# Layer 1's linear attention: q formed transposed and squared at eviction, its norm applied at the output rows, x (Wv W_out) in one product with k

## The chip, the cores and the metric

The kernel runs on one core of one Trainium2 chip. The metric is the device time of one execution in microseconds. The median of three timed runs of the kernel before is 815.91 us (812.31 to 816.70). Engines are named as in the profile: PE is TensorE (PEld its weight loads), DVE is VectorE, ACT is ScalarE, POOL is GpSimd, SP is the queue from which most DMAs are issued.

## The reference

The program is a small vision tower: a tokenizer, then layer 0 (attention and a mixture of six experts), then layer 1 (linear attention and a gated mixture with a shared MLP). The change is in the linear attention of layer 1:

```python
def _L1_attn_ref(x, W_qkv, b_qkv, W_out, b_out):
    b, N, C = x.shape
    qkv = x @ W_qkv + b_qkv
    q, k, v = jnp.split(qkv, 3, axis=2)
    q = q - jnp.mean(q, axis=2, keepdims=True)
    k = k - jnp.mean(k, axis=2, keepdims=True)
    q2 = q * q
    k2 = k * k
    q2s = jnp.sum(q2, axis=2, keepdims=True)
    k2s = jnp.sum(k2, axis=2, keepdims=True)
    k2 = _l2_normalize(k2 / (k2s + EPS_DIV), axis=-2)
    q2 = _l2_normalize(q2 / (q2s + EPS_DIV), axis=-1)
    kv = jnp.einsum('bnc,bnd->bcd', k2, v)
    t2 = jnp.einsum('bnc,bcd->bnd', q2, kv) / math.sqrt(N)
    attn = v + t2
    return attn @ W_out + b_out
```

Here x is the layer norm of h, and the result is added to h. There are 4 images; each has 2352 tokens that are three equal copies of 784, so the kernel computes 784 rows per image and writes each three times. C is 256. Everything is float32; a product of the code appears as two matmuls in the trace.

Two facts are used. Since q2 is normalised along its own row, dividing it by its sum first changes almost nothing, and its norm is one number per token. And (v + t2) W_out is x (Wv W_out) plus q2 (kv W_out) plus constants, so v itself need not be formed.

## The kernel before

The 28 tiles of 112 tokens (TT) are cut into eight units, for each image one of four tiles and one of three (`units`); the odd units have three. The names below stand with their lines in the kernel before.

- `fetch(u)` (L1360) gathers the experts' rows of unit u from DRAM, one indirect DMA of GpSimd per tile and choice; `stats_one` and `normalise` (L1383 to L1406) add them to h, take the statistics and write the normalised rows `xa`; `residual` (L1413) adds the constant row `bres` to h. `ys`, the gathered rows, has three buffers.
- `x_t(u)` transposes `xa` on TensorE (`pt`, L297) and copies the result to `lxT` (half on ScalarE, L81, half on VectorE, L83).
- `q_k(u, j0, j1)` multiplies each tile by the centred 512 columns of q and k (`pqk`, L1574). VectorE adds the bias (L1578); ScalarE squares both halves with a row sum (L1582) and squares q's half once more into `junk` for the sum of fourth powers (L1583).
- `scales(u)` takes the root of that sum (L1598) and the reciprocals (L1602), multiplies k's half on ScalarE into `uk` (L1606) and q's half on VectorE in place (L1607), and squares `uk` into `sq` (L1611). `fold(u)` adds `sq` up (L1618 to L1623).
- `q_t(u)` transposes q (`pt<-ident,qk`, L297) and copies it to `lqT`.
- `k_x(b)`, once an image: the column norms `pn`, `kn` (L1635 to L1642), the product `pukx` of uk with the rows xa (L1648) and its scaled copy `g` (L1652). `g_t(b)` turns g (`pgT`, L1662, copied at L1665); `kv_out(b)` multiplies it by Wvo (`pkvo`, L1674) and writes `kvo` on VectorE (L1678).
- `rows_out(u)`: for two tiles at a time one PSUM tile `pout` takes lxT times Wvo (L1689) and, on top, lqT times kvo (L1694); VectorE adds it to h (L1700).
- `layer1_weights()` makes Wvo = Wv W_out and the constant row: transposes `pwv` (L598), a copy `WvT` on VectorE (L602), products `pwvo` (L607), copies `Wvo` on ScalarE (L611), and the bias part `pbvo` (L618 to L621). It is called in step u = 1, after that unit's q and k.

A loop over u = 0 to 9 strings these together; a unit's rows go out two steps after its q and k were made. In this stage the order of the instructions on each engine is made by a scheduler, from the program's order and its own estimate of when operands are ready; it is fixed when the kernel is built. The expert blocks just before (`hidden`, `rows_back`, L1165 to L1199) have the order of VectorE and of the SP queue written out by hand; `centred_weights()` is called in them. PSUM has a pool of seven banks (`ps_tile`) and one further bank (`psum_s`, one buffer) for `pn` and the small gate products.

Of the kernel before, what the change touches and what calls it, by code (L numbers as in the profile page):

```python
# [60 lines left out]
def tile_vit_tower(ctx: ExitStack, tc: tile.TileContext, a: dict, out: bass.AP):  # L61
# [515 lines left out]
    def centred_weights():  # L577
        qkw = Wqkv[:, :, : 2 * D].rearrange("p c (i d) -> p c i d", i=2)
        mean = w1p.tile([P, 2, 2], F32, tag="mean", name="mean")
        nc.vector.tensor_reduce(mean, qkw, AX.X, ALU.add)  # L580
        nc.vector.tensor_scalar(mean, mean, 1.0 / D, None, ALU.mult)
        nc.vector.tensor_tensor(
            qkw, qkw, mean.unsqueeze(3).to_broadcast([P, 2, 2, D]), ALU.subtract
        )
        qkb = bqkv[:, : 2 * D].rearrange("p (i d) -> p i d", i=2)
        meanb = w1p.tile([TT, 2], F32, tag="meanb", name="meanb")
        nc.vector.tensor_reduce(meanb, qkb, AX.X, ALU.add)
        nc.vector.tensor_scalar(meanb, meanb, 1.0 / D, None, ALU.mult)
# [749 lines left out]
    bout = spread(w1p, "bout", a["L1_attn_b_out"], nc.sync)  # L1338

# [94 lines left out]
    with tc.manual_schedule(engines={mybir.EngineType.DVE, mybir.EngineType.SP}):  # L1434
        own_weights(NEARLY)
        turned(NEARLY)
        for i in range(NEARLY, NBLK + 1):
# [117 lines left out]
    lin = linear.enter_context(tc.tile_pool(name="lin", bufs=2, reuse_waits="tile"))  # L1555
    sumsof = {}

    def q_k(u, j0, j1):

        n = units[u][2]  # L1560
        xT = xTs[u]
        if j0 == 0:
            qks[u] = lin.tile([TT, GT, 2 * D], F32, tag="qk", name="qk")
            sumsof[u] = (
                small.tile([TT, GT, 2], F32, tag="ss", name="ss"),
                small.tile([TT, GT], F32, tag="s4", name="s4"),
            )
        qk = qks[u]
        ss, s4 = sumsof[u]
        junk = lin.tile([TT, D], F32, tag="junk", name="junk", bufs=1)  # L1570
        for j in range(j0, min(j1, n)):
            pqk = ps_tile("pqk")[:TT]
            for c in range(2):
                nc.tensor.matmul(  # L1574
                    pqk, xT[:, c, cut(j, 1)], Wqkv[:, c, : 2 * D],
                    start=(c == 0), stop=(c == 1),
                )
            nc.vector.tensor_tensor(qk[:, j, :], pqk, bqkv[:, : 2 * D], ALU.add)  # L1578

            for i in range(2):  # L1580
                half = qk[:, j, i * D : (i + 1) * D]
                nc.scalar.activation(half, half, AF.Square, accum_out=ss[:, j, i : i + 1])  # L1582
            nc.scalar.activation(junk, qk[:, j, :D], AF.Square, accum_out=s4[:, j : j + 1])  # L1583
            if u:
                stats_one(u + 1, j)
        if j1 >= n and u:
            if u + 1 < len(units) and units[u + 1][2] > n:
                stats_one(u + 1, n)
            normalise(u + 1)

    def scales(u):

        b, j0, n = units[u]
        qk = qks[u]
        ss, s4 = sumsof.pop(u)

        nc.vector.tensor_scalar(ss[:, :n], ss[:, :n], 1e-7, None, ALU.add)
        nc.scalar.activation(s4[:, :n], s4[:, :n], AF.Sqrt, bias=zero[:TT])  # L1598
        nc.vector.scalar_tensor_tensor(
            ss[:, :n, 0], ss[:, :n, 0], 1e-12, s4[:, :n], ALU.mult, ALU.max  # L1600
        )
        nc.vector.reciprocal(ss[:, :n], ss[:, :n])  # L1602
        uk = uks[u] = lin.tile([TT, GT, D], F32, tag="uk", name="uk", bufs=3)
        sq = lin.tile([TT, GT, D], F32, tag="sq", name="sq", bufs=1)
        for j in range(n):
            nc.scalar.activation(uk[:, j, :], qk[:, j, D:], AF.Copy, scale=ss[:, j, 1:2])  # L1606
            nc.vector.tensor_scalar(  # L1607
                qk[:, j, :D], qk[:, j, :D], ss[:, j, 0:1], None, ALU.mult
            )
        for j in range(n):  # L1610
# [3 lines left out]
    def fold(u, sq):  # L1614
# [4 lines left out]
        else:  # L1619
# [62 lines left out]
    def rows_out(u):  # L1682
        b, j0, n = units[u]
        xT, qT, kvo = xTs.pop(u), qTs.pop(u), kvos[b]
        for two in halves(range(n)):
            pm = ps_tile("pout")[:TT].rearrange("p (t d) -> p t d", t=2)
            for i, j in enumerate(two):
                for c in range(2):
                    nc.tensor.matmul(  # L1689
                        pm[:, i, :], xT[:, c, cut(j, 1)], Wvo[:, c, :],  # L1690
                        start=(c == 0), stop=False,
                    )
                for c in range(2):
                    nc.tensor.matmul(  # L1694
                        pm[:, i, :], qT[:, c, cut(j, 1)], kvo[:, c, :],
                        start=False, stop=(c == 1),
                    )
# [7 lines left out]
    for u in range(len(units) + 2):  # L1705
        b, odd = divmod(u - 2, 2)
        one_image = u >= 2 and not odd
        if u == 0:
            fetch(3)
            x_t(1)  # L1710
            q_k(0, 0, GT)
            squares[0] = scales(0)
            fold(0, squares.pop(0))
            continue
        if u < len(units):
# [3 lines left out]
        if one_image:  # L1719
            k_x(b)  # L1720
            q_t(u - 1)
        if u == 2:
# [129 lines left out]
```

## Time and profile before

| | us |
|---|---|
| timed runs, median of 3 (lowest, highest) | 815.91 (812.31, 816.70) |
| the profiled execution's own time | 849.85 |
| its span, first to last instruction | 848.1 |

The profiled execution's mean granted TensorE clock is 0.954 of full speed. By stretches of the trace, TensorE is busy for 335 of the first 400 us, 108 of the 110 between 400 and 510, and 137 of the last 144 (the gated mixture). The linear attention of layer 1 lies between about 518 and 704 us.

Some groups of that stage (busy us in all, mean ns of one):

| line | engine | what | count | busy us | mean ns |
|---|---|---|---|---|---|
| L1574 | PE | pqk, 512 columns | 112 | 50.0 | 595 |
| L1689 | PE | pout from Wvo, 256 columns | 107 | 27.8 | 380 |
| L1694 | PE | pout from kvo, 256 columns | 104 | 27.1 | 382 |
| L1648 | PE | pukx, 258 columns | 112 | 29.0 | 415 |
| L1582 | ACT | Square of q and of k with row sum | 56 | 22.8 | 407 |
| L1583 | ACT | Square for the fourth powers | 28 | 11.3 | 402 |
| L1578 | DVE | bias added to q and k, 512 columns | 28 | 19.2 | 688 |
| L1607 | DVE | q scaled, 256 columns | 28 | 8.2 | 353 |

Busy times on one engine overlap: matmuls are pipelined, and an instruction's end reaches into the next one's start. The distance from start to start is what a long row of them costs. A few matmul records are missing from the trace (112 would be expected for both rows of pout).

### The profile page before, as it was taken

The page shows a single profiled execution, that of the slowest core. Times are in us where ns is not written, and L with a number is a line of the kernel's source. Part 1 is how long each engine was busy: PE and PEld are TensorE (multiplying, and loading weights), DVE is VectorE, ACT ScalarE, POOL GpSimd, SP SyncE. Part 2 cuts the span into 40 slices and gives each one's busy share as a digit, 9 for nine tenths or more (in the row PEclk, how much of TensorE's full clock was granted, in tenths as well). Part 3 has the DMA queues.
Part 4 walks back from the last instruction along what each step waited for, and adds up shares of the span by engine and source line. Part 5 has one row for each costly group of instructions (what it writes and reads, how often), then busy time and mean ns, then how long its engine had stood idle before and what let it go on. Part 6 is the DMA issues. An engine that isn't in the chain of part 4 may idle for free. (4 is left out here: it accounts for less than half of the span.)

```text
span 848.1 us, 11129 instructions
## 1 busy us (share of the span) xinstructions
PE 746.0 (88%) x3669; PEld 525.4 (62%) x3669; DVE 515.1 (61%) x1619; ACT 318.2 (38%) x758; POOL 129.3 (15%) x151
## 2 busy tenths in 40 slices
PE   2879988999788788799999999348999999999996
PEld 2758765555465466678878885335767675555553
DVE  4369886585787874346445655358995745544441
ACT  1333535455547573242222323323564612222221
POOL 5100000000024605430030022744000000000000
PEclk9999999999999988799999999759999999999999
DMA  8999990000001293332342224311000001333333
GB/s 197 360 421 419 419 384 0 1 0 1 1 22 55 82 367 95 103 127 75 100 131 88 94 88 137 93 52 55 1 2 0 1 3 27 100 101 101 99 100 100
DMA packets 58286, 97.52 MB, mean 115 GB/s; under 512 B 14590, under 2 KB 48564, under 8 KB 53364
## 3 DMA queue, kind: packets, MB, share of 16 engines
q1 hardware_dynamic: 51100, 80.78, 27.7%
q0 software_dynamic: 6224, 14.13, 5.8%
q10 hardware_dynamic: 904, 1.89, 0.9%
q8 instruction: 29, 0.48, 0.2%
q14 instruction: 29, 0.24, 0.1%
HBM read 31.04 MB, written 65.74 MB: 114 GB/s over the span
## 5 line engine op out<-in xcount | busy, mean ns | idle before, releaser
L901 POOL DMA_INDIRECT xrows<-xn,pos x56 | 59.9, 1070 | 282.4 <-ACT kq L665 233.2
L1369 POOL DMA_INDIRECT ys<-yrows,pos x56 | 54.3, 969 | 163.5 <-DMA yrows<-yb 134.0
L1173 PE MATMUL pb<-xTb,own 128*128 128x256 f32 x240 | 60.3, 396 | 7.0 <-DVE hb L1181 2.1
L1190 PE MATMUL pyb<-own,hb 128*128 128x256 f32 x240 | 59.4, 392 | 4.4 <-ACT hb L1179 4.4
L1173 PE MATMUL pb<-hb,own 128*128 128x256 f32 x240 | 58.8, 388 | 0.3 <-DVE hb L1181 0.3
L1179 ACT ACTIVATE hb<-pb,own 128x256 f32<-128x256 f32 x74 | 34.7, 473 | 61.7 <-PE pb L1173 42.1
L1173 PEld LDWEIGHTS pb<-xTb,own 128*128 128x128 f32 x240 | 45.5, 198 | 16.7 <-ACT xTb L1163 3.8
L1190 PEld LDWEIGHTS pyb<-own,hb 128*128 128x128 f32 x240 | 46.9, 197 | 12.0 <-ACT hb L1179 5.2
L297 PE MATMUL pt<-ident,xn 112*128 112x112 f32 x280 | 42.2, 281 | 12.4 <-DVE xn L482 6.9
L1574 PE MATMUL pqk<-Wqkv,lxT 128*112 128x512 f32 x112 | 50.0, 595 | 0.5 <-ACT lxT L81 0.5
L297 PEld LDWEIGHTS pt<-ident,xn 112*128 112x128 f32 x280 | 32.4, 148 | 26.4 <-issue 9.1
L1173 PEld LDWEIGHTS pb<-hb,own 128*128 128x128 f32 x240 | 44.5, 195 | 6.2 <-DVE hb L1181 0.7
L1196 DVE TENSOR_TENSOR yb<-pyb,eb 128x512 f32<-128x512 f32 x30 | 20.7, 691 | 45.5 <-PE pyb L1190 35.3
L306 PE MATMUL pe<-xT,eW 128*128 128x448 f32 x112 | 45.2, 546 | 0.0
L1648 PE MATMUL pukx<-xa,uk 112*128 112x258 f32 x112 | 29.0, 415 | 18.5 <-ACT uk L1606 18.5
L1163 ACT COPY xTb<-ptb 128x512 f32<-128x512 f32 x30 | 17.5, 583 | 73.8 <-PE ptb L1159 65.2
L1181 DVE TENSOR_SCALAR hb<-pb,own 128x256 f32<-128x256 f32 x46 | 22.2, 482 | 30.9 <-PE pb L1173 29.6
L1648 PEld LDWEIGHTS pukx<-xa,uk 112*128 112x128 f32 x112 | 22.7, 208 | 22.3 <-issue 18.8
L317 PE MATMUL pwo<-Wo,oT 128*112 128x256 f32 x112 | 29.0, 413 | 7.6 <-DVE oT L730 6.7
L1574 PEld LDWEIGHTS pqk<-Wqkv,lxT 128*112 128x112 f32 x112 | 19.2, 177 | 25.2 <-issue 22.7
L690 DVE SCALAR_TENSOR_TENSOR prod<-kq 128x784 f32<-128x784 f32 x32 | 30.4, 971 | 7.2 <-ACT kq L665 5.0
L1582 ACT ACTIVATE qk<-qk 112x256 f32<-112x256 f32 x56 | 22.8, 407 | 28.1 <-DVE qk L1578 23.8
(339 smaller groups left out, 1525.4 us busy)
## 6 DMA issues: line engine op xcount, KB each, us to landing
xrows<-nothing SPq DMA_DIRECT2D x19, 1024.0 KB
yrows<-nothing SPq DMA_DIRECT2D x19, 1024.0 KB
out_dram<-h SPq DMA_DIRECT2D x26, 336.0 KB
xb<-xrows SPq DMA_DIRECT2D x30, 256.0 KB
yrows<-yb SPq DMA_DIRECT2D x30, 256.0 KB
ew<-in_L_ffn_expert_w_dram SPq DMA_DIRECT2D x6, 768.0 KB
wb<-wd SPq DMA_DIRECT2D x28, 112.0 KB
img<-in_x_dram ACTq DMA_DIRECT2D x2, 588.0 KB
```

The lines of the kernel that those rows point to most:

```text
L297: nc.tensor.transpose(pt[:, j * TT : (j + 1) * TT], xn[:, j, c * P : (c + 1) * P], ident[:TT, :TT])
L306: nc.tensor.matmul(pm[: wcols.stop - wcols.start, :n], w[:, c, wcols], xT(c), start=(c == 0), stop=(c == chunks - 1),)
L317: nc.tensor.matmul(pm[:, i, :], xT(c, t), w[:, c, :], start=(c == 0), stop=(c == chunks - 1))
L690: nc.vector.scalar_tensor_tensor(prod, qTs[s][:, o, :], 1.0, kT[:, o, t * SEQ : (t + 1) * SEQ], ALU.mult, ALU.mult, accum_out=atts[s][:, o ...
L901: put = nc.gpsimd.indirect_dma_start(out=xrows[:, :], out_offset=bass.IndirectOffsetOnAxis(ap=pos[:, k, t0 + j : t0 + j + 1], axis=0), in_ ...
L1173: nc.tensor.matmul(pm, wm[:, c, o * P : (o + 1) * P], src[:, c, :], start=(c == 0), stop=(c == 1),)
L1179: nc.scalar.activation(dst[:, o, :], pm, AF.Relu, bias=b)
L1190: nc.tensor.matmul(pm[:, t, :], src[:, c, t * P : (t + 1) * P], wm[:, c, :], start=(c == 0), stop=(c == 1),)
L1369: got = nc.gpsimd.indirect_dma_start(out=y[:, j, k, :], out_offset=None, in_=yrows[:, :], in_offset=bass.IndirectOffsetOnAxis(ap=pos[:, k, ...
L1574: nc.tensor.matmul(pqk, xT[:, c, cut(j, 1)], Wqkv[:, c, : 2 * D], start=(c == 0), stop=(c == 1),)
L1582: nc.scalar.activation(half, half, AF.Square, accum_out=ss[:, j, i : i + 1])
L1648: nc.tensor.matmul(pg, uks[u][:, k, c * P : (c + 1) * P], xas[u % 4][:, k, : D + 2], start=(j == 0), stop=(j == TPI - 1),)
```

## The change

q and k are no longer one product.

- `k_of(u)` makes k alone. In unit 0, where Wvo doesn't exist yet, it is a product of 256 columns for two tiles at a time; in all later units one of 512 columns, 256 of k and 256 of x Wvo. For this Wvo is kept in the place of Wv in `Wqkv`. VectorE adds k's bias and, in a second instruction, adds the x Wvo half straight to h. Of the Squares with row sum one is left per tile (k's).
- `q_of(u)` makes q transposed (the weights' columns are stationary, lxT moves): two halves of 128 rows by up to 448 tokens. ScalarE evicts each with a Square and a bias column `bq` into `lqT`; one more Square makes `q4`. The transposes of q, their copies and q's scaling on VectorE are gone.
- `norms(u)` sums q4 over the 256 channels with a matrix of ones, four tiles in the four quarters of one PSUM tile, copies it out on ScalarE, turns it with a small matmul, and takes root, maximum and reciprocal into `rq`, one number per token. It is called one step later.
- `rows_out(u)` keeps only the product of lqT with kvo; VectorE multiplies it by rq and adds it to h, tile by tile. Unit 0 alone still does its x Wvo product there.
- `layer1_weights` is called in step 0 instead of step 1, its copy `WvT` moves from VectorE to ScalarE, and its bias columns `bvs` are made earlier (`bias_columns`, in the expert blocks, where `centred_weights` now also makes `bq`).

```diff
--- before.py
+++ after.py
@@ -589,8 +589,21 @@
         nc.vector.tensor_tensor(
             qkb, qkb, meanb.unsqueeze(2).to_broadcast([TT, 2, D]), ALU.subtract
         )
-    def layer1_weights():
+        pb = ps_tile("pbq")
+        for c in range(2):
+            nc.tensor.matmul(
+                pb[:, c : c + 1], bqkv[:1, c * P : (c + 1) * P], ones[:1], start=True, stop=True
+            )
+        nc.vector.tensor_copy(bq, pb[:, :2])
+    def bias_columns():
+        bvs = w1p.tile([P, 2, P], F32, tag="bvs", name="bvs")
+        for k in range(2):
+            nc.vector.tensor_copy(bvs[:, k, :], col("bv", k).to_broadcast([P, P]))
+        return bvs
+    def layer1_weights(bvs):
         WvT = w1p.tile([P, 2, D], F32, tag="WvT", name="WvT")
         pt = ps_tile("pwv").rearrange("p (k i) -> p k i", k=2)
         for k in range(2):
@@ -599,8 +612,8 @@
                     pt[:, k, c * P : (c + 1) * P],
                     Wqkv[:, c, 2 * D + k * P : 2 * D + (k + 1) * P], ident,
                 )
-        nc.vector.tensor_copy(WvT, pt)
-        Wvo = w1p.tile([P, 2, D], F32, tag="Wvo", name="Wvo")
+        nc.scalar.copy(WvT, pt)
+        Wvo = Wqkv[:, :, 2 * D :]
         for c in range(2):
             pw = ps_tile("pwvo")[:, :D]
             for k in range(2):
@@ -609,9 +622,6 @@
                     start=(k == 0), stop=(k == 1),
                 )
             nc.scalar.copy(Wvo[:, c, :], pw)
-        bvs = w1p.tile([P, 2, P], F32, tag="bvs", name="bvs")
-        for k in range(2):
-            nc.vector.tensor_copy(bvs[:, k, :], col("bv", k).to_broadcast([P, P]))
         bvo = w1p.tile([P, D], F32, tag="bvo", name="bvo")
         pw = ps_tile("pbvo")[:, :D]
         for k in range(2):
...
+    bq = w1p.tile([P, 2], F32, tag="bq", name="bq")
...
@@ -1445,6 +1460,7 @@
                 hidden(i, 1)
             if i == NEARLY + 1:
                 centred_weights()
+                bvs = bias_columns()
             for u in range(3):
                 if i - 1 == after[u]:
                     fetch(u)
@@ -1553,60 +1569,92 @@
     late = [early]
 
     lin = linear.enter_context(tc.tile_pool(name="lin", bufs=2, reuse_waits="tile"))
-    sumsof = {}
-    def q_k(u, j0, j1):
-        n = units[u][2]
+    sumsof, q4s, rqs, with_v = {}, {}, {}, set()
+    ones32 = lin.tile([P, 32], F32, tag="ones32", name="ones32", bufs=1)
+    nc.vector.memset(ones32, 1.0)
+    def k_of(u):
+        b, j0, n = units[u]
+        if lw:
+            with_v.add(u)
         xT = xTs[u]
...
+        kr = qks[u] = lin.tile([TT, GT, D], F32, tag="kr", name="kr")
+        ss = sumsof[u] = small.tile([TT, GT], F32, tag="ss", name="ss")
+        for two in halves(range(n)):
+            if not lw:
+                pk = mm_rows(two, lambda c, j: xT[:, c, cut(j, 1)], Wqkv[:, :, D : 2 * D], "pk")
+                nc.vector.tensor_tensor(
+                    kr[:, two[0] : two[-1] + 1, :], pk, over(bqkv[:, D : 2 * D], len(two)),
+                    ALU.add,
+                )
+            for j in two:
+                if lw:
+                    pk = ps_tile("pk")[:TT]
+                    for c in range(2):
+                        nc.tensor.matmul(
+                            pk, xT[:, c, cut(j, 1)], Wqkv[:, c, D:], start=(c == 0), stop=(c == 1)
+                        )
+                    nc.vector.tensor_tensor(kr[:, j, :], pk[:, :D], bqkv[:, D : 2 * D], ALU.add)
+                    ht = h[:, b * TPI + j0 + j, :]
+                    nc.vector.tensor_tensor(ht, pk[:, D:], ht, ALU.add)
+                nc.scalar.activation(
+                    kr[:, j, :], kr[:, j, :], AF.Square, accum_out=ss[:, j : j + 1]
+                )
+                if u:
+                    stats_one(u + 1, j)
+        if u:
             if u + 1 < len(units) and units[u + 1][2] > n:
                 stats_one(u + 1, n)
             normalise(u + 1)
 
+    def q_of(u):
+        n = units[u][2]
+        qT = qTs[u] = lin.tile([P, 2, GN], F32, tag="lqT", name="lqT", bufs=4)
+        q4 = q4s[u] = lin.tile([P, 2, GN], F32, tag="q4", name="q4", bufs=1)
+        for o in range(2):
+            pq = mm_t(
+                n * TT, Wqkv, slice(o * P, (o + 1) * P), lambda c: xTs[u][:, c, : n * TT], "pq1"
+            )
+            nc.scalar.activation(qT[:, o, : n * TT], pq, AF.Square, bias=bq[:, o : o + 1])
+        nc.scalar.activation(q4[:, :, : n * TT], qT[:, :, : n * TT], AF.Square)
+    def norms(u):
+        n = units[u][2]
+        q4 = q4s.pop(u)
+        pg = psum_s.tile([P, 512], F32, tag="pss", name="pq4")[: 32 * n, :TT]
+        for c in range(2):
+            for j in range(n):
+                nc.tensor.matmul(
+                    pg[32 * j : 32 * (j + 1), :], ones32, q4[:, c, cut(j, 1)],
+                    start=(c == 0), stop=(c == 1),
+                )
+        qn = small.tile([P, TT], F32, tag="qn", name="qn", bufs=2)[: 32 * n]
+        nc.scalar.copy(qn, pg)
+        pr = psum_s.tile([P, 512], F32, tag="pss", name="pqn")[:TT, :n]
+        nc.tensor.matmul(
+            pr, qn, ident.rearrange("p (j e) -> p j e", e=32)[: 32 * n, :n, 0],
+            start=True, stop=True,
+        )
+        r = rqs[u] = small.tile([TT, GT], F32, tag="rq", name="rq", bufs=4)
+        nc.scalar.activation(r[:, :n], pr, AF.Sqrt, bias=zero[:TT])
+        nc.vector.tensor_scalar(r[:, :n], r[:, :n], 1e-19, None, ALU.max)
+        nc.vector.reciprocal(r[:, :n], r[:, :n])
     def scales(u):
 
         b, j0, n = units[u]
-        qk = qks[u]
-        ss, s4 = sumsof.pop(u)
+        kr = qks.pop(u)
+        ss = sumsof.pop(u)
         nc.vector.tensor_scalar(ss[:, :n], ss[:, :n], 1e-7, None, ALU.add)
-        nc.scalar.activation(s4[:, :n], s4[:, :n], AF.Sqrt, bias=zero[:TT])
-        nc.vector.scalar_tensor_tensor(
-            ss[:, :n, 0], ss[:, :n, 0], 1e-12, s4[:, :n], ALU.mult, ALU.max
-        )
         nc.vector.reciprocal(ss[:, :n], ss[:, :n])
         uk = uks[u] = lin.tile([TT, GT, D], F32, tag="uk", name="uk", bufs=3)
         sq = lin.tile([TT, GT, D], F32, tag="sq", name="sq", bufs=1)
         for j in range(n):
-            nc.scalar.activation(uk[:, j, :], qk[:, j, D:], AF.Copy, scale=ss[:, j, 1:2])
-            nc.vector.tensor_scalar(
-                qk[:, j, :D], qk[:, j, :D], ss[:, j, 0:1], None, ALU.mult
-            )
+            nc.scalar.activation(uk[:, j, :], kr[:, j, :], AF.Copy, scale=ss[:, j : j + 1])
         for j in range(n):
             nc.scalar.activation(sq[:, j, :], uk[:, j, :], AF.Square)
         return sq
@@ -1621,11 +1669,6 @@
             nc.vector.tensor_tensor(acc, acc, sq[:, 0:2, :], ALU.add)
             nc.vector.tensor_tensor(acc[:, 0, :], acc[:, 0, :], sq[:, 2, :], ALU.add)
             nc.vector.tensor_tensor(acc[:, 0, :], acc[:, 0, :], acc[:, 1, :], ALU.add)
-    def q_t(u):
-        n = units[u][2]
-        qT = qTs[u] = lin.tile([P, 2, GN], F32, tag="lqT", name="lqT", bufs=3)
-        transposed(qks.pop(u), n, lambda c, pt: copy_out(qT[:, c, : n * TT], pt))
 
     def k_x(b):
 
@@ -1681,23 +1724,18 @@
 
     def rows_out(u):
         b, j0, n = units[u]
-        xT, qT, kvo = xTs.pop(u), qTs.pop(u), kvos[b]
+        xT, qT, kvo, r = xTs.pop(u), qTs.pop(u), kvos[b], rqs.pop(u)
         for two in halves(range(n)):
...
             t = b * TPI + j0 + two[0]
             ht = h[:, t : t + len(two), :]
-            nc.vector.tensor_tensor(ht, pm[:, : len(two), :], ht, ALU.add)
+            if u not in with_v:
+                pm = mm_rows(two, lambda c, j: xT[:, c, cut(j, 1)], Wvo, "pxo")
+                nc.vector.tensor_tensor(ht, pm, ht, ALU.add)
+            pq = mm_rows(two, lambda c, j: qT[:, c, cut(j, 1)], kvo, "pqo")
+            for i, j in enumerate(two):
+                nc.vector.scalar_tensor_tensor(
+                    ht[:, i, :], pq[:, i, :], r[:, j : j + 1], ht[:, i, :], ALU.mult, ALU.add
+                )
@@ -1708,9 +1746,12 @@
         if u == 0:
             fetch(3)
             x_t(1)
-            q_k(0, 0, GT)
+            k_of(0)
+            q_of(0)
             squares[0] = scales(0)
             fold(0, squares.pop(0))
+            lw.extend(layer1_weights(bvs))
+            Wvo, bvo = lw[:2]
             continue
         if u < len(units):
             fetch(u + 3)
@@ -1718,21 +1759,20 @@
             shared = shared1(0)
         if one_image:
             k_x(b)
-            q_t(u - 1)
+        if u == len(units):
+            norms(u - 1)
         if u == 2:
             gT = g_t(0)
             kv_out(0, gT)
             rows_out(0)
             x_t(2)
         if u < len(units):
-            q_k(u, 0, 2)
+            k_of(u)
+            norms(u - 1)
         if one_image and b:
             gT = g_t(b)
         if u < len(units):
-            q_k(u, 2, GT)
-            if u == 1:
-                lw.extend(layer1_weights())
-                Wvo, bvo = lw[:2]
+            q_of(u)
             squares[u] = scales(u)
         if one_image and b:
             kv_out(b, gT)
@@ -1743,14 +1783,12 @@
         if 2 <= u < len(units) - 1:
             x_t(u + 1)
         if u == 3:
-            for k in range(3):
+            for k in range(2):
                 residual(k)
         if u >= 2 and (b or odd):
             rows_out(u - 2)
         if u < len(units):
             fold(u, squares.pop(u))
-            if u % 2:
-                q_t(u - 1)
     linear.close()
 
     with tc.tile_pool(name="ffn1", bufs=2) as work:
```

More of the change, by code (lines that the diff above doesn't have):

```diff
@@ L1555, in tile_vit_tower @@
     lin = linear.enter_context(tc.tile_pool(name="lin", bufs=2, reuse_waits="tile"))
-    sumsof = {}
-    def q_k(u, j0, j1):
-        n = units[u][2]
-        xT = xTs[u]
[L1562 to L1566, printed above, removed]
-            )
-        qk = qks[u]
[L1569 to L1576, printed above, removed]
-                )
[L1578 to L1586, printed above, removed]
@@ L1589, in q_k @@
             normalise(u + 1)
+    def q_of(u):
[29 more added lines that the diff above has]
+        nc.vector.reciprocal(r[:, :n], r[:, :n])
     def scales(u):
         b, j0, n = units[u]
-        qk = qks[u]
-        ss, s4 = sumsof.pop(u)
+        kr = qks.pop(u)
+        ss = sumsof.pop(u)
         nc.vector.tensor_scalar(ss[:, :n], ss[:, :n], 1e-7, None, ALU.add)
-        nc.scalar.activation(s4[:, :n], s4[:, :n], AF.Sqrt, bias=zero[:TT])
-        nc.vector.scalar_tensor_tensor(
-            ss[:, :n, 0], ss[:, :n, 0], 1e-12, s4[:, :n], ALU.mult, ALU.max
-        )
         nc.vector.reciprocal(ss[:, :n], ss[:, :n])
@@ L1605, in scales @@
         for j in range(n):
-            nc.scalar.activation(uk[:, j, :], qk[:, j, D:], AF.Copy, scale=ss[:, j, 1:2])
-            nc.vector.tensor_scalar(
-                qk[:, j, :D], qk[:, j, :D], ss[:, j, 0:1], None, ALU.mult
-            )
+            nc.scalar.activation(uk[:, j, :], kr[:, j, :], AF.Copy, scale=ss[:, j : j + 1])
         for j in range(n):
@@ L1683, in rows_out @@
         b, j0, n = units[u]
-        xT, qT, kvo = xTs.pop(u), qTs.pop(u), kvos[b]
+        xT, qT, kvo, r = xTs.pop(u), qTs.pop(u), kvos[b], rqs.pop(u)
         for two in halves(range(n)):
[L1686 to L1697, printed above, removed]
             t = b * TPI + j0 + two[0]
             ht = h[:, t : t + len(two), :]
-            nc.vector.tensor_tensor(ht, pm[:, : len(two), :], ht, ALU.add)
+            if u not in with_v:
[6 more added lines that the diff above has]
+                )
     squares = {}
```

## The prediction

> **What bounds the kernel now.** I read the busy shares and the 40 slices first, then a table of stretches over the linear-attention stage (about 518 to 704 us), then the chain of waits there, then TensorE's and ScalarE's timelines at the head of the stage.
>
> ```profile
> span 848.1 us, 11129 instructions
> PE 746.0 (88%) x3669; PEld 525.4 (62%) x3669; DVE 515.1 (61%) x1619; ACT 318.2 (38%) x758; POOL 129.3 (15%) x151
> ```
>
> ```profile
> 530.00:540.00 10.00, 4.16 (x13) 3.12 (x12) 7.36 (x23) 6.34 (x24) 7.56 (x9) 0.71 0.30 89
> 540.00:550.00 10.00, 4.19 (x21) 3.25 (x20) 0.58 (x2) 0.70 (x3) 7.56 (x9) 0.84 0.34 96
> 550.00:560.00 10.00, 0.00 (x0) 0.00 (x0) 3.10 (x11) 0.83 (x3) 5.03 (x6) 0.50 0.27 77
> ...
> 580.00:600.00 20.00, 19.47 (x73) 10.73 (x72) 19.71 (x49) 11.01 (x43) 6.05 (x6) 1.00 0.12 35
> 600.00:640.00 40.00, 40.00 (x179) 28.54 (x178) 38.48 (x120) 23.40 (x89) 0.00 (x0) 1.00 0.00 1
> 640.00:680.00 40.00, 40.00 (x189) 27.20 (x188) 24.73 (x78) 21.62 (x72) 0.00 (x0) 1.00 0.00 1
> ```
>
> Columns after start and length: busy us of PE, PEld, DVE, ACT, POOL, then the granted clock and DMA. From 580 on TensorE never rests (40.00 of 40); VectorE is close behind until 640 (19.71 of 20, 38.48 of 40, though an instruction's busy time overlaps the next one's). Between 530 and 560 all three compute engines idle while GpSimd gathers.
>
> ```profile
> 592.56 0.42 ACT lxT L81
> 593.03 5.40 PE pqk L1574 x12
> 598.43 0.77 PE pt L297 x8
> 599.20 0.87 PE pout L1689 x4
> 600.07 0.86 PE pout L1694 x4
> ```
>
> ```profile
> 530.16 0.60 PE L598 MATMUL pwv<-ident,Wqkv 128*128 128x128 f32 x4
> 536.61 3.78 PE L607 MATMUL pwvo<-Wout,WvT 128*128 128x256 f32 x8 [5.84 <-issue]
> 562.65 3.78 PE L1648 MATMUL pukx<-xa,uk 112*128 112x258 f32 x8 [18.46 <-ACT uk L1606]
> ```
>
> ```profile
> 545.38 0.42 ACT L1583 ACTIVATE junk<-qk 112x256 f32<-112x256 f32 x1 [5.48 <-remote]
> 551.71 0.30 ACT L1598 ACTIVATE s<-s,zero 112x3 f32<-112x3 f32 x1 [5.63 <-remote]
> 561.57 0.53 ACT L81 COPY lqT<-pt 128x448 f32<-128x448 f32 x1 [9.03 <-remote]
> ```
>
> The chain runs PE to PE; its steps are my prices: pqk 1.717 a 112-token tile (5.15 for three), a unit's eight transposes 0.77, each half of pout 0.865 a tile. Before 562 TensorE waits 18.46 us for uk, because ScalarE stands still 5.5, 5.6 and 9.0 us on signals whose work was long done: its lqT copy waits to 561.57 for transposes finished at 542.4.
>
> This profiled execution took 849.85, the timed ones 815.91 in the median: 34 less. The 18.46 and the clock of 0.5 to 0.84 round it are the obvious candidates, so I sum without this gap and add the difference to the median.
>
> [...] the slices after the gaps at 530 and 544 have 0.71 and 0.50. [...]
>
> **The change, part by part.** Times are TensorE's unless said.
>
> Work per tile. Gone: q's half of pqk, 0.858, and q's transposes, 0.193. New: q formed transposed, as heavy as a unit's "ps L306 x8" of 3.02 us in the chain, so 0.755; the norm's sums, like "pgate L1513 x16" at 0.52 a unit, 0.13; the small turn pqn, an estimate of 0.2 a unit, 0.05. x(Wv W_out) only moves from pout into the 512-wide product. Net 0.116 a tile: 3.2 us over 28 tiles, 0.8 of it in units 0 and 1, 2.4 in units 2 to 7. [...]
>
> ScalarE loses three Squares with accumulator a tile (0.40 each in sequence) and half the lqT copies, gains one such Square, two evictions of 448 and one Square of 896 a unit. VectorE: 0.60 + 0.28 + 0.30 + 0.13 before, by start-to-start distances in its timeline (qk add, q scale, h add, lqT copy), and 0.33 + 0.33 + 0.39 plus 0.08 after. Both get lighter: cost nothing, with TensorE full above them.
>
> Head. In the built order of the changed kernel, unit 1's product needs Wvo; Wvo's copies stand on ScalarE behind unit 2's rstd, which needs unit 2's last statistics. On VectorE these are behind the first adds of unit 3's gathered rows. In the trace that point is 537.2 to 537.4, so unit 1's product starts at about 537.7. Before, it was finished at 530.2, and TensorE waited only for WvT (536.6). Before, without the gap: pwvo and pbvo end at 541.5, then transposes and the pukx-to-pkvo sequence, 10.3 in the last image (680.76 to 691.10): first rows out at 552.6. After: 537.7 + 5.15 (pk) + 2.26 (q) + 0.1 + 10.3 + about 1.0 (waits for uk and for the pqn turn) = 556.5, plus 0.6 for a half clock after the idling: 557.1. That is 4.5 late, less 2.6 of pout (three tiles of 0.865) already done: +1.9, which contains the 0.8. Bounds: -3 if Wvo comes as early as TensorE could take it (532), +6 with the full half clock and slower gathers.
>
> Between units 2 and 3. Here the order puts unit 2's norm sums ahead of unit 3's product. They need the Square of 896 on ScalarE: after the last q product come eviction 0.75 with latency, a uk of 0.40[...], 2.0 against 0.57 of transposes: about 1.5 idle. Queued behind that Square are two uk (0.8), four sq (1.33, the "sq" row's 0.33 apart) and the lxT copy (0.65 with latency) for which unit 3's product waits: 2.8 against 0.45 of sums, 2.3 idle. Before, the lxT copy stood ahead of the last tile's Squares and cost 0.24. Sum 3.7, bounds 0 to 4.5; half clock from it 0.4, bounds 0 to 1.7.
>
> kvo. rows_out now begins with the product that needs kvo; before, 0.86 of pout L1689 covered VectorE's two kvo (0.48 each). Uncovered in the last image 0.65, about 0.1 in two others: 0.9, bounds 0 to 1.5. The pqn turn waits for a ScalarE copy queued behind Squares: 0.2 twice, 0.4, bounds 0 to 1.2. Its PSUM bank (one buffer, also for pn and the gates) is held through that turn; the next user is TensorE itself, several us later. Nobody waits for pqn for long: its scale is used a unit later.
>
> One answer each, nothing: the bias columns and the two tiny bq products (under 0.3, beside full TensorE work in the expert blocks); no DMA and no GpSimd instruction is added or moved; table loads stay two in the linear stage (an Exp, a Sqrt).
>
> Sum: +1.9 - 2.4 + 3.7 + 0.4 + 0.9 + 0.4 = +4.9. On the profiled execution's 849.85 that is 854.8; on the median, 820.8. I say 821.0, its own range 816 to 827.
>
> **The rivals.** (1) The waits are mostly covered. The place is the same, but half of the 3.7 and all of the head's 1.9 vanish because ScalarE runs ahead: +4.9 - 1.9 - 1.9 = +1, so 817. For it: ScalarE's load falls. Against it: the 3.7 hangs on a chain that starts with TensorE's own last q product, so no head start helps.
>
> (2) Faster: VectorE sets the pace from 578 to 640. It does 15 tiles there, and 1.31 - 1.13 = 0.18 a tile from the sums above, 2.7, plus the 3.2 of TensorE, give -5.9 when the new waits fall where TensorE waited for VectorE anyway: 810. For it: 19.71 of 20 and 38.48 of 40. Against it: TensorE's 40.00 of 40 and a chain that leaves it for 2.5 us only. It decides if TensorE idles under 1.5 us between units 2 and 3.
>
> (3) Much slower: the gap belongs to the timed executions too. Then the added hops (WvT, Wvo, unit 1's product, its Square) sit in the stretch where a signal takes over 5 us, and unit 1's 7.4 us of products come after 562 instead of before: +4.9 + 7 = 828. Against it are the 34 us.
>
> **How the numbers follow.** Forecast 0.50, (1) 0.16, (2) 0.22, (3) 0.12. About 0.5%, 4.1 us, is what a measurement of this kernel can tell from no change: 811.8 to 820.0. Seven tenths of the forecast lie above 820.0 (0.35) and all of (3): slower 0.47. Three tenths of the forecast and most of (1): same 0.28. (2) and the rest of (1): faster 0.25. Leaving out half of (2) below and a third of (3) above, with the far end of the forecast, gives 809 to 831.
>
> **What would show it.** In the changed profile: q by L306 at 3.02 us a full unit; no transposes of qk; pk starting after 537 us behind a Wvo copy; TensorE idle of 1 to 2.5 us twice between units 2 and 3, released by q4 and by lxT; a wait for kvo of about 0.65 in the last image. If the two idles are absent, the forecast is wrong by 4; if the median falls by more than 4, VectorE was the bound.

## The result, and the profile after

Medians: 822.31 us for the changed kernel (four runs, 821.33 to 826.03), 814.11 for the kernel before (four runs, 810.64 to 816.70). The ratio is 1.0125, with a 95% interval of 1.0091 to 1.0159. The two medians lie 8.2 us apart, the ratio makes it 10.2 us (7.4 to 12.9). The profiled execution of the changed kernel took 821.33 itself, so it stands for the timed ones, unlike the one of before (849.85).

The first two lines of the page of the changed kernel:

```profile
span 819.6 us, 11144 instructions
PE 735.9 (90%) x3713; PEld 513.9 (63%) x3713; DVE 507.3 (62%) x1622; ACT 312.4 (38%) x677; POOL 132.2 (16%) x151
```

The table of stretches of the changed kernel over the linear stage (start, length, busy us of PE, PEld, DVE, ACT, POOL, then clock and DMA):

```profile
520.00:530.00 10.00, 6.57 (x30) 4.35 (x31) 6.39 (x20) 3.31 (x11) 7.50 (x9) 0.67 0.33 93
530.00:540.00 10.00, 10.00 (x30) 5.59 (x29) 9.96 (x34) 4.67 (x14) 7.63 (x8) 0.89 0.31 88
...
573.00:613.00 40.00, 40.00 (x175) 24.70 (x174) 28.88 (x92) 16.37 (x50) 0.00 (x0) 1.00 0.00 1
```

As before, TensorE rests mostly at the head of the stage. New are two idles between units 2 and 3 (experiment 4); from 573 to the end of the stage at 675 it waits twice, 0.36 us in all. The last row begins 15 us after unit 2's first k product, as the row 600:640 of the kernel before does after its product of q and k. In these 40 us VectorE was busy for 38.48 and is now busy for 28.88, while TensorE is busy for 40.00 in both: the relief of VectorE bought nothing there.

The large new thing lies 130 us ahead of this stage, in the expert blocks. TensorE's timeline of the changed kernel there (start, length, instruction; in brackets the idle before it and what ended it):

```profile
375.85 1.89 PE L1183 MATMUL pb<-hb,own 128*128 128x256 f32 x8
382.44 1.01 PE L594 MATMUL pbq<-ones,bqkv 1*128 1x1 f32 x4 [4.70 <-DVE bqkv L589]
383.38 3.78 PE L1183 MATMUL pb<-xTb,own 128*128 128x256 f32 x8
386.95 2.85 PE L1200 MATMUL pyb<-own,hb 128*128 128x256 f32 x8
389.64 0.60 PE L1169 MATMUL ptb<-ident,xb 128*128 128x128 f32 x4
```

And VectorE's timeline in the same place:

```profile
377.78 0.48 DVE L1191 TENSOR_SCALAR hb<-pb,own 128x256 f32<-128x256 f32 x1 [0.43 <-PE pb L1183]
378.18 1.21 DVE L580 TENSOR_REDUCE mean<-Wqkv 128x4 f32<-128x1024 f32 x1
...
379.63 1.23 DVE L582 TENSOR_TENSOR Wqkv<-Wqkv,mean 128x1024 f32<-128x1024 f32 x1
...
381.69 0.69 DVE L589 TENSOR_TENSOR bqkv<-bqkv,meanb 112x512 f32<-112x512 f32 x1
```

The two tiny products pbq read the centred bias. VectorE begins the centring only when the block's last ReLU (hb) is done, at 378.18, and is through 4.2 us later; TensorE has nothing left ahead of pbq from 377.74. It waits 4.70 us with the whole next block queued behind. The eight matmuls of pb then take 3.78 us, twice the 1.89 of the eight of the same shape above them: the idle has cost the clock as well.

The table of stretches of the changed kernel at this place shows that too (0.53 is the clock):

```profile
376.00:382.40 6.40, 1.74 (x9) 1.18 (x7) 5.73 (x9) 1.06 (x2) 0.00 (x0) 0.97 0.26 82
382.40:389.30 6.90, 6.86 (x19) 5.72 (x20) 0.91 (x4) 0.47 (x1) 0.00 (x0) 0.53 0.00 0
```

The profiles of this and the next four kernels repeat a stretch of the same code to within a microsecond, so the loss can be laid out by place. The distances below are from start to start on TensorE, in us: from the last pmeta (L949) in the expert blocks to the first product of the linear stage; from there to unit 2's first k product (the head); from there to the feed-forward layer's first pe (units 2 to 7); the rest. The only profiles of the kernel before have the gap of about 18 us in the head, so its row is that of the kernel before with pbq added (experiment 3), whose linear stage is the old one.

| kernel | expert blocks | head | units 2 to 7 | rest |
|---|---|---|---|---|
| before, with pbq added (experiment 3) | 151.25 | 44.63 | 118.69 | 144.42 |
| changed | 151.21 | 49.47 | 117.47 | 144.42 |
| changed, pbq without its wait (experiment 1) | 144.19 | 48.90 | 117.85 | 144.42 |
| changed, pbq moved to the head (experiment 2) | 144.12 | 48.57 | 117.88 | 144.49 |
| changed, unit 3's transposes earlier (experiment 4) | 151.27 | 48.59 | 114.63 | 144.46 |

So the change costs 7.0 in the expert blocks (151.21 against 144.19, which stands for the old blocks, an estimate since no kernel without pbq has an undisturbed profile), 4.8 at the head, and gives back 1.2 in units 2 to 7: 10.6 us, where the ratio says 10.2 (0.0125 of 814.11).

### The profile page after: what moved, and what is told of

Its sections match the earlier page's. It is cut to its first block, busy times and chain, and to the rows that moved or that the text cites. A ratio compares the mean times of both kernels' runs of the same rounds, so it can differ in the third digit from the quotient of the medians.

```text
span 819.6 us, 11144 instructions
## 1 busy us (share of the span) xinstructions
PE 735.9 (90%) x3713; PEld 513.9 (63%) x3713; DVE 507.3 (62%) x1622; ACT 312.4 (38%) x677; POOL 132.2 (16%) x151
## 3 DMA queue, kind: packets, MB, share of 16 engines
q10 hardware_dynamic: 904, 1.89, 1.0%
## 5 line engine op out<-in xcount | busy, mean ns | idle before, releaser
L1384 POOL DMA_INDIRECT ys<-yrows,pos x56 | 56.9, 1016 | 150.0 <-DMA yrows<-yb 133.9
L1183 PE MATMUL pb<-hb,own 128*128 128x256 f32 x240 | 56.8, 380 | 0.0
L1595 PE MATMUL pk<-Wqkv,lxT 128*112 128x512 f32 x96 | 44.3, 614 | 3.9 <-ACT lxT L81 2.0
L1595 PEld LDWEIGHTS pk<-Wqkv,lxT 128*112 128x112 f32 x96 | 17.3, 182 | 26.9 <-issue 20.1
L306 PEld LDWEIGHTS pe<-xT,eW 128*128 128x128 f32 x112 | 20.2, 190 | 20.9 <-issue 20.9
L1160 DVE COPY own<-ew 128x1540 f32 x30 | 29.0, 968 | 4.9 <-issue 1.3
L1398 DVE SCALAR_TENSOR_TENSOR h<-ys,wk,h 112x256 f32<-112x256 f32 x56 | 25.8, 472 | 8.5 <-DMA ys<-yrows,pos 8.3
```

The source lines that it names most:

```text
L306: nc.tensor.matmul(pm[: wcols.stop - wcols.start, :n], w[:, c, wcols], xT(c), start=(c == 0), stop=(c == chunks - 1),)
L1160: nc.vector.tensor_copy(w, ewf[0][:, bass.ds(off, EW)])
L1183: nc.tensor.matmul(pm, wm[:, c, o * P : (o + 1) * P], src[:, c, :], start=(c == 0), stop=(c == 1),)
L1384: got = nc.gpsimd.indirect_dma_start(out=y[:, j, k, :], out_offset=None, in_=yrows[:, :], in_offset=bass.IndirectOffsetOnAxis(ap=pos[:, k, ...
L1398: nc.vector.scalar_tensor_tensor(h[:, t, :], ys[u][:, j, k, :], wk[:, k, t : t + 1], h[:, t, :], ALU.mult, ALU.add,)
L1595: nc.tensor.matmul(pk, xT[:, c, cut(j, 1)], Wqkv[:, c, D:], start=(c == 0), stop=(c == 1))
```

## The experiments

Theory A: the wait of pbq delays everything behind it and is the larger half of the loss. Theory B: the linear stage is all of the loss, since its head waits for gathered rows anyway and eats up what is lost before it.

**1. The wait alone taken away** (`bq_no_wait`). The products read a row that has long been loaded.

```diff
-                pb[:, c : c + 1], bqkv[:1, c * P : (c + 1) * P], ones[:1], start=True, stop=True
+                pb[:, c : c + 1], bout[:1, c * P : (c + 1) * P], ones[:1], start=True, stop=True
```

> The changed kernel, except that the two small products pbq read the row of bout (there since its load) in place of the centred row of bqkv; every instruction stands where it stood on every engine, only TensorE's wait for VectorE is gone. The bias that goes into q is thereby another one. Theory A (the wait of pbq in the expert blocks, 4.70 us of idle and the half clock of 6.83 us after it, delays everything behind it): about 7 us less than the changed kernel, so about 815, a ratio of 1.002 to the kernel before, no idle at pbq and a clock of 1.00 from 382 to 389. Theory B (the linear-attention stage costs all of the loss, since its start waits for the gathered rows anyway): at most 2 us less, 820 or more, with the time that is won at pbq lost again at the head of the stage.

Measured: 817.59 us, ratio 1.0066 (1.0032 to 1.0099). TensorE's timeline of that kernel:

```profile
378.39 1.89 PE L1183 MATMUL pb<-hb,own 128*128 128x256 f32 x8
380.21 0.60 PE L594 MATMUL pbq<-ones,bout 1*128 1x1 f32 x4
380.74 2.00 PE L1183 MATMUL pb<-xTb,own 128*128 128x256 f32 x8
382.57 1.89 PE L1200 MATMUL pyb<-own,hb 128*128 128x256 f32 x8
384.30 0.60 PE L1169 MATMUL ptb<-ident,xb 128*128 128x128 f32 x4
```

Same instructions, same order on every engine, no wait: pbq costs its 0.5 us, the matmuls behind it are back at 2.00 and 1.89 (granted clock 1.00 from 377 to 390), and the expert blocks are 7.02 us shorter. From pbq to ptb it is 4.09 us here and 7.20 with the wait, so about 3.1 of the price is the half clock. Wait and clock make 7.8; 0.8 of it comes back further on, where small waits of this kernel, such as 0.43 for own at 387.26, are missing in the changed one. What was won stays won: the head and the units behind it are as long as in the changed kernel to within 0.6. Theory B falls by the trace. The timed runs alone would not decide it: the ratio went from 1.0125 to 1.0066, which is 4.8 us and not the 7 that Theory A put, the intervals overlap, and the 1.002 that it named lies outside.

**2. pbq moved to the head of the stage** (`bq_in_head`).

```diff
             k_of(0)
+            q_bias()
             q_of(0)
```

> The changed kernel with pbq and its copy to bq moved from the expert blocks to the head of the linear stage, between unit 0's k and q products; it computes the same. Theory A: about 7 us less than the changed kernel, 815, as in the run without the wait, because the centred bias is long there and pbq costs 0.3 us. Theory B: at most 2 us less.

Measured: 816.70 us, ratio 1.0057 (1.0037 to 1.0077); expert blocks 144.12. The repair is worth 0.68% by the two ratios, 5.5 us, and 7.1 in the trace; the 815 of Theory A was missed by 1.7.

**3. pbq alone added to the kernel before** (`before_with_bq`).

```diff
+        pb = ps_tile("pbq")
+        for c in range(2):
+            nc.tensor.matmul(
+                pb[:, c : c + 1], bqkv[:1, c * P : (c + 1) * P], ones[:1], start=True, stop=True
+            )
+        nc.vector.tensor_copy(bq, pb[:, :2])
```

> The kernel before with nothing but pbq and its copy added behind the centring in the expert blocks (nobody reads bq). Theory A: about 7 us more than the kernel before, 821, a ratio near 1.009, with an idle of 4 to 5 us at pbq. Theory B: at most 2 us more.

Measured: 822.74 us, ratio 1.0088 (1.0053 to 1.0123). TensorE's timeline of that kernel:

```profile
382.79 1.89 PE L1179 MATMUL pb<-hb,own 128*128 128x256 f32 x8
389.38 1.01 PE L594 MATMUL pbq<-ones,bqkv 1*128 1x1 f32 x4 [4.69 <-DVE bqkv L589]
390.32 3.78 PE L1179 MATMUL pb<-xTb,own 128*128 128x256 f32 x8
```

As Theory A said, the time is near 821 and the idle between 4 and 5 us: six lines whose arithmetic is two columns cost this kernel 0.9%, 7.2 us. The same profile gives the old head, which the one of before hid behind its gap:

```profile
515.25 12.18 PE L1581 MATMUL pqk<-Wqkv,lxT 128*112 128x512 f32 x28
527.27 0.60 PE L604 MATMUL pwv<-ident,Wqkv 128*128 128x128 f32 x4
535.25 3.78 PE L613 MATMUL pwvo<-Wout,WvT 128*128 128x256 f32 x8 [7.38 <-DVE WvT L608]
...
540.70 5.40 PE L1655 MATMUL pukx<-xa,uk 112*128 112x258 f32 x24
```

One wait of 7.38 us, for WvT. In the changed kernel TensorE's timeline shows three in its place, and unit 1's product behind them (pq<-q,ones are unit 0's norm sums; the tile of fourth powers bears the name q in the traces):

```profile
508.27 3.62 PE L317 MATMUL pk<-Wqkv,lxT 128*112 128x256 f32 x16
...
519.89 0.98 PE L1631 MATMUL pq<-q,ones 128*32 128x112 f32 x16 [4.56 <-ACT q L1621]
522.38 3.48 PE L620 MATMUL pwvo<-Wout,WvT 128*128 128x256 f32 x8 [1.52 <-ACT WvT L615]
...
528.64 7.10 PE L1595 MATMUL pk<-Wqkv,lxT 128*112 128x512 f32 x12 [1.91 <-ACT Wqkv L624]
```

The three waits sum to 7.99 us, only 0.6 more than the old one. So most of the 4.84 us by which the head is longer is work that stands in it now, such as unit 1's x Wvo (2.6 us by the prediction's price), and the clock, halved here from 528.84 to 532.25: unit 1's product took 7.10 us here and 5.40 in the kernels of experiments 1 and 2, whose heads are 0.6 and 0.9 shorter.

**4. Unit 3's transposes ahead of unit 2's q** (`x3_before_q2`), against the two idles between these units. In the changed kernel TensorE's timeline has them so:

```profile
567.70 0.74 PE L297 MATMUL pt<-ident,xa 112*128 112x112 f32 x6
569.82 0.59 PE L1631 MATMUL pq<-q,ones 128*32 128x112 f32 x16 [1.38 <-ACT q L1621]
572.17 5.40 PE L1595 MATMUL pk<-Wqkv,lxT 128*112 128x512 f32 x12 [1.75 <-ACT lxT L81]
```

```diff
+        if u == 2:
+            x_t(3)
         if u < len(units):
             q_of(u)
```

> The changed kernel with unit 3's transposes put ahead of unit 2's q products, so that the lxT copy no longer stands behind the Square of 896, and the built order puts unit 3's k product ahead of unit 2's norm sums. Both theories: the two idles of 1.38 and 1.75 us between units 2 and 3 go, 2 to 3.1 us less than the changed kernel, 819 to 820. If ScalarE or VectorE were the bound there, the idle would come back further on and the time stay within 1 us.

Measured: 822.47 us, ratio 1.0100 (1.0073 to 1.0127). TensorE's timeline of that kernel:

```profile
570.63 0.74 PE L297 MATMUL pt<-ident,xa 112*128 112x112 f32 x6
571.21 3.19 PE L306 MATMUL pq<-lxT,Wqkv 128*128 128x448 f32 x8
574.23 5.31 PE L1595 MATMUL pk<-Wqkv,lxT 128*112 128x512 f32 x12
579.47 0.59 PE L1631 MATMUL pq<-q,ones 128*32 128x112 f32 x16
```

Both idles are gone and do not return: units 2 to 7 take 114.63 instead of 117.47, so 2.84 us. The timed runs do not confirm it: the median did not fall, and the two ratios' intervals overlap. The profiled execution shows where such a gain can be lost: it came to the last pmeta 6.3 us later than that of the changed kernel (363.38 against 357.06), in code that is the same in both. The mean granted clocks of the six runs were 0.962 to 0.965, those of the changed kernel's four 0.965 to 0.968; whether that is chance or comes with this kernel isn't shown.

**5. The kernel before again, and combinations.** From here on every kernel, the kernel before included, took about 40 us more. The runs fall into sessions, each made on one chip: experiments 1 to 4 in one, with 813.26 for the kernel before, the runs below in three, with 854.01, 853.09 and 851.00. The first of these three was on the same chip as experiments 1 to 4, the others on two other chips. The ratios below stand beside each other, not beside those above.

> The kernel before, unchanged, profiled once more. If the gap of 18.46 us in front of pukx is a thing of that one profiled execution: no such gap, the linear stage (from the first pqk to the feed-forward layer's first pe) about 163 us instead of 185.6, as in the run with pbq added, and 144 us from the last pmeta to the stage. If the gap belongs to the kernel (the prediction's rival 3): it is there again, with the stage over 180 us.

Measured: 854.58 us, with the gap and a stage of 189.1 us, as TensorE's timeline shows:

```profile
545.25 1.92 PE L1648 MATMUL pukx<-xa,uk 112*128 112x258 f32 x8
564.84 1.63 PE L1648 MATMUL pukx<-xa,uk 112*128 112x258 f32 x3 [17.67 <-ACT uk L1606]
```

and VectorE's timeline one of the waits that stand behind it, a small instruction held for 11.56 us while GpSimd issues gathers. "Remote" is a signal whose sender the profile does not name:

```profile
551.14 0.23 DVE L1597 TENSOR_SCALAR ss<-ss 112x6 f32<-112x6 f32 x1 [11.56 <-remote]
```

By the wording of the expectation the gap belongs to the kernel. But the same kernel ran at 813.26 one session earlier, and all kernels that ran here are slower by as much: the gap goes with whole sessions.

> The changed kernel with both edits, pbq in the head and unit 3's transposes ahead of unit 2's q products. Theory A with the two idles added as it is (7.0 us in the expert blocks and 3.7 in the linear stage, which are all of the loss): about 10.7 us less than the changed kernel, the same as the kernel before within 1.5 us, 812 to 815; 144.1 us from the last pmeta to the stage, and a stage of about 163. If the timed run with unit 3's transposes moved, which won nothing, is to be believed: 816 to 817, as with pbq moved alone.

> The kernel of bq_head_x3 once more, since that call's chip ran every kernel some 40 us slower than the chips before, the kernel before included, with the gap of about 18 us at the head of the linear stage. If the chip is one of the faster kind (kernel before near 813): Theory A with the two idles gives 812 to 815, a ratio of 0.998 to 1.003, a stage of about 163 us and 144.1 us from the last pmeta to the stage. If the gain of unit 3's transposes is lost again: 816 to 817. On a chip of the slower kind: a ratio near 1.006 again.

Edits 2 and 4 together: 859.45 us, ratio 1.0064 (1.0035 to 1.0094), and again 861.00, 1.0091 (1.0055 to 1.0126). Units 2 to 7 took 114.20 both times, 4.5 less than the 118.70 of the kernel before in `before_again`; the head took 70.59 and 77.58 against 70.42. The same kernel's head differs by 7 us between the two sessions. With such heads the sum can't be tested; that the two edits bring the change level with the kernel before in a session like the first (144.12 + 48.57 + 114.20 + 144.4 = 451.3 from the last pmeta, against about 451.9 for the kernel before, its 458.99 less 7.1) is an estimate from the table's rows, not measured.

`bq_head_wvo_early` makes Wvo in the expert blocks, so that unit 0 has the 512-column product too; the call in step 0 and the two residuals of step 3 go, since `normalise` then adds them. `all_three` adds edit 4.

```diff
                 bvs = bias_columns()
+            if i == NEARLY + 2:
+                lw.extend(layer1_weights(bvs))
+                Wvo, bvo = lw[:2]
```

> The changed kernel with pbq in the head, and the products for Wv W_out taken from the head of the linear stage into the expert blocks (one block after the centring); unit 0 also gets them in its 512-column product. Theory H1 (the head is late because unit 1's product waits for Wvo's copies, which stand on ScalarE behind unit 2's rstd and so behind the gathered rows): 5.1 us of products and 2.9 us of waits leave the head, the stage falls from 166.4 to about 159, the expert blocks grow from 144.1 by 4.6 for the products and about 1.5 for one wait for WvT: about 2 us less than with pbq moved alone, 814 to 815. Theory H2 (the gathered rows themselves bound the head): the stage falls by less than 3 us, the expert blocks grow by the same 6, and the time is 3 us more, 820.

> The three edits together. Theories A and H1: 0 to 4 us less than the kernel before, 809 to 813. Theory H2: 3 us more than the kernel before, 816.

> The kernel of all_three once more, for the same reason. On a chip of the faster kind: Theory H1: 0 to 4 us less than the kernel before, the stage about 156 and the expert blocks about 150. Theory H2 (the gathered rows bound the head): 2 to 4 us more than the kernel before.

> The kernel of all_three a last time, to have it on a chip of the faster kind if this call gets one. There: by Theory H1 0 to 4 us less than the kernel before (ratio 0.995 to 1.000), the stage about 156 to 159 us against 163.3 of the kernel before and 166.4 with pbq in the head alone, and about 150 from the last pmeta to the stage; by Theory H2 2 to 4 us more than the kernel before. On a chip of the slower kind: a ratio of 1.002 to 1.003, as twice before.

Measured: 858.87 us, 1.0038 (1.0012 to 1.0065) for the first; for the three of `all_three` 855.87, 855.71 and 851.32, ratios 1.0023 (0.9999 to 1.0047), 1.0029 (1.0008 to 1.0050) and 1.0019 (0.9997 to 1.0041). It is the best of the combinations and still not ahead of the kernel before. Its head, 71.23, 70.49 and 70.66, is no shorter than that of edits 2 and 4 (70.59) although the products for Wvo have left it; that of `bq_head_wvo_early` is 67.59. ScalarE's timeline of `all_three_again` shows the longest wait:

```profile
567.12 0.25 ACT L1641 COPY qn<-pq 128x112 f32<-128x112 f32 x1 [21.32 <-remote]
```

The sums pq that this copy reads were done at 540. The same wait is 21 to 22 us long in all four profiles with Wvo made early. In these sessions, then, the head hangs on a late signal and no longer on Wvo; H1 and H2 stay open, since no session like the first came to test them.

**6. VectorE's order by hand** (`dve_by_hand`), on top of `all_three`.

> The kernel of all_three with VectorE's instructions of the linear stage kept in the order in which they are written, where each add of gathered rows stands behind an add of unit 1's k, and the last of unit 2's rows and its normalisation behind unit 1's scales. Theory H2' (the order on VectorE, which puts adds that wait for gathered rows ahead of unit 0's and unit 1's scales, is what holds ScalarE and then TensorE at the head): no idle at unit 0's norm sums, the first rows out about 28 to 32 us after the start of the stage instead of 40, and 5 to 9 us less than all_three. If the gathers themselves bound it, or if the order by hand puts new waits between the units: within 2 us of all_three, or more.

Measured: 867.68 us, ratio 1.0178 (1.0135 to 1.0220), the worst of all. The head is 8.6 us shorter than in `all_three_again` (61.90 against 70.49), but ScalarE still waits 19.43 us for "remote" at the same copy, and the first rows come out 57.3 us after the start of the stage, not the 28 to 32 of H2' (65.9 in `all_three_again`). And units 2 to 7 take 138.17 instead of 114.22. TensorE's timeline shows two of the new waits:

```profile
598.53 0.38 PE L297 MATMUL pt<-ident,xa 112*128 112x112 f32 x2 [3.02 <-DVE xa L1423]
...
615.75 1.98 PE L297 MATMUL pt<-ident,xa 112*128 112x112 f32 x8 [4.91 <-DVE xa L1423]
```

In the order as written the rows of the next unit are normalised too late for its transposes. H2' did not come true here; whether it would without the late signals is not tested, and a rewrite that fixes only the head's order wasn't tried.

## Why the prediction was right or wrong

The sign, the range and, within 1.3 us, the time came out; that the time came so near was partly luck. The sum was +4.9 on 815.91. Measured is +8.2 by the medians, +10.2 by the ratio and +10.6 by the stretches, so about twice the sum, and it started from a kernel before that now ran at 814.11, 1.8 lower. By place the prediction had 0 for the expert blocks, +4.5 for the head and +0.4 for units 2 to 7; the traces have +7.0, +4.8 and -1.2.

- **The step that failed** is "One answer each, nothing: the bias columns and the two tiny bq products (under 0.3, beside full TensorE work in the expert blocks)". The work is indeed half a microsecond; experiment 1 shows that the wait is the cost, 4.70 us of idle and 3.1 of half clock, 7.0 net. The prediction's own lines have ScalarE standing still for 5.48, 5.63 and 9.03 us at one instruction each, and yet it did not ask what pbq waits for and who stands behind it. The built order had the answer: pbq ahead of the next block's pb, and on VectorE the centring behind the last ReLU of the same block.
- **Head**: 4.5 late predicted, 4.84 measured (49.47 against 44.63). Unit 1's product was put 19.6 us after the stage's first product and came 20.4 after it, behind the copy of Wvo, as said. A wait of 4.56 for unit 0's norm sums was not foreseen; it lies ahead of the wait for Wvo, inside the same stretch. That the gathers hold VectorE's queue and with it ScalarE's is read from the traces, not shown by an experiment: in the changed kernel VectorE's first add of gathered rows there waits 3.04 us for its DMA, the reciprocal ss stands behind two such adds, and ScalarE's uk waits 3.50 us for ss; its rstd waits 5.55 us for mv.
- **Units 2 to 3**: idles of 1.5 and 2.3, less 0.24, predicted (together 3.6, where the prediction wrote 3.7); 1.38 and 1.75 found, released by q and by lxT as named, and worth 2.84 in the trace when removed. How long the Square of 896 in the 1.5 takes, no trace of before shows; at 568.83 in the changed kernel it takes 0.94 us, and the next instruction starts 0.84 after it. The half clock of 0.4, an estimate, did not come: the granted clock was 1.00 from 560 to 675.
- **kvo**: 0.9 predicted, none found. In the last image pkvo starts at 666.56 and runs 1.99, and the product that needs kvo starts at 668.39 without a wait.
- **pqn**: 0.4 predicted; a wait of 0.36 for qn in the first image, none later. The table loads stayed two in the stage, 1.28 us each.
- **Work**: 2.6 for unit 1's rows and 2.4 for the other units predicted to go from units 2 to 7, 5.0 in all; with edit 4, which leaves no wait there, the stretch is 4.06 shorter than the old one (114.63 against 118.69).
- **The rivals.** (1), waits mostly covered, is refuted by the idles. (2), VectorE as the bound, needed less than 1.5 us of idle between units 2 and 3; there were 3.13, the median did not fall, and VectorE's relief from 38.48 to 28.88 of 40 left TensorE at 40.00. (3) had the right doubt and the wrong alternative: the 34 us were not in the executions timed then, yet whole later sessions had them.

## What to carry to other kernels

Here two matmuls of one column cost what they waited for, 4.70 us with the whole queue behind them, plus about 3.1 for the clock that fell during the wait. Before an instruction is booked as nothing, look up where the built order puts it on its engine, and when its operand's engine gets to writing that operand; if in doubt, put it where the operand is long finished. And where runs scatter by more than the effect, compare the lengths of the same stretch in several traces: within the first session they repeat to within one microsecond, while the time to the last pmeta scatters by six.

## What the runs showed of the hardware

Two executions of the same code, the tokenizer at the start, got different clocks. The table of stretches of the changed kernel:

```profile
40.00:60.00 20.00, 15.27 (x75) 11.60 (x74) 14.32 (x49) 5.65 (x10) 0.00 (x0) 0.94 1.01 426
```

and of the kernel with unit 3's transposes earlier:

```profile
40.00:60.00 20.00, 16.30 (x58) 12.13 (x56) 11.59 (x40) 1.94 (x4) 0.00 (x0) 0.74 1.01 426
```

TensorE had the same idles of 2.2 and 2.9 us in both. In the first they cost no clock; in the second the clock was halved for 3.41 us from 40.38 and for 6.83 us from 47.20: its rows of 16 and of 14 pw there took 5.39 and 5.02 us against 3.71 and 3.19, and its first pwp came at 55.19 instead of 49.94 (52.21 in the kernel of experiment 1, 50.02 in that of experiment 2). What decides between the two, no run isolates. In the changed kernel the clock was halved for 3.41 us from 57.80, after idles of no more than 0.63. In its trace all changes of the clock lie whole multiples of 3.41 us apart. How much idle it takes stays open: TensorE was busy for 2.03 of the 3.41 us ahead of that fall, and for 1.87 of the 3.41 us up to 47.56, three such steps earlier, where none followed.

The other surprise is the sessions in which everything takes 40 us more. In them, engines wait 5 to 22 us for signals whose sender the profile does not name, while GpSimd issues its gathers one every 1.23 us, as in the first session. What brings this condition about stays open; the same chip had been without it one session earlier.
